# Where the second attention's weights and its first batch's pieces stand in the program

## The chip, the cores and the metric

The kernel runs on one core of a Trainium2 chip. Its time is the device time of one execution in microseconds (us), the median of several runs. The core has five engines with a queue each: PE multiplies matrices into PSUM, DVE, ACT and POOL work on vectors, SP issues transfers (DMA). PEld is PE's loading of the stationary operand. Each engine works through its own list of instructions in the order in which the list was written.

## The reference

Four batches of 512 rows of 128 numbers pass through a macaron: half a mixture of experts, linear attention, half a mixture of experts, half a block of six layers, softmax attention, and half a second block of the same six layers. The steps around the change are the end of the first block and the softmax attention:

```python
x = x + 0.5 * _L1_ffn_ref(_layernorm(x), ...)                 # six layers: local attention + gated FFN
x = x + _L1_attn_ref(_layernorm(x), W_Q, W_K, W_V, W_K_prime, W_O, alpha)
x = x + 0.5 * _L1_ffn_ref(_layernorm(x), ...)

def _L1_attn_ref(x, W_Q, W_K, W_V, W_K_prime, W_O, alpha):     # 16 heads of 8
    q, k, v, kp = (_heads(x @ W.T) for W in (W_Q, W_K, W_V, W_K_prime))
    out_std = softmax(q @ k.T / sqrt(8)) @ v
    out_p   = softmax(q @ kp.T / sqrt(8)) @ v
    return merge(alpha * out_std + (1 - alpha) * out_p) @ W_O.T
```

## The kernel before

The program is written in four parts: 0 the front (experts and linear attention), 1 the first block of layers, 2 the softmax attention, 3 the second block. Each piece of work is a Python generator whose steps are put on a list with a time (`Events.at`, L546); a step may name others that it must follow, and is then put just behind the latest of them, however early its own time was. A part is written out in the order of these times (`run`, L566). In parts 1 and 3 that order is kept on every engine (`manual_schedule`, L1387). In parts 0 and 2 a planner in the build orders the instructions, and it may move those of part 2 up among the last of part 1.

**The end of part 1.** A layer has two units of heads per batch (projections L299, norms L336 and L371, scores L434, softmax L457, values L416 and L482) and a gated FFN per batch (`Ffn`, L628). In the last layer of the block, the block's input is read back from DRAM into the one tile `xo` (`aside`, L731; L734 is the transfer), and `fadd` (L723) adds the FFN's output (L726) and then half of the sum to `xo` (L728). The time of `aside` (19.734, L611) puts the four pairs of `aside` and `fadd` behind everything else of part 1. Until its `fadd`, a batch's FFN output stays in one of the four PSUM banks "mm" (L68, L716).

**The softmax attention** (`l1_attn`, L1114).

- `weights` (L1119) loads four matrices of 128x128, one DMA each into `wr`, which has two buffers (L1122), and splits each into a high part on ACT (L854) and a low part on DVE (L855). W_O and alpha are loaded behind them.
- `prep` (L1153) makes one batch ready: a layer norm (L92 to L110), a transposition on PE (L860), a split (L854, L855), then for Q, K and K' three matmuls into a bank (`mm3`), three bf16 pieces of the result (`pc`, two buffers; ACT L1166, DVE L1167, ACT L1168, DVE L1169), and three DMAs that write them to DRAM (`pd`, L1173). V follows (L1177 to L1184).
- `first` (L1277) runs `prep(0)` and reads the pieces back, spread over heads, into the tiles of queries and keys (`load`, L1147: four DMAs each, L1151; `stack`, L1131, fills the unused rows).
- `slots` (L1326) then runs 32 units of four heads. A slot takes the row maxima of a new unit (16 matmuls L1200 into three banks in turn, each reduced on DVE, L1201), and, from the third slot on, scores, exponentials and averages of the unit that started two slots earlier (`LAG`, L1225 to L1241). `prep` of a later batch is fed in a step at a time (L1303).

Where they are put is said in four lines:

```python
ev.at(t0 - P["w"], (key, "w"), weights)                                   # L1339
ev.row(t0, P["dp"], names, first(), {names[0]: [(key, "w")] + ready[0:1], names[5]: memory[0:1]})
ready = l1_attn(..., ready=[((5, b), "fadd", 0) for b in range(4)],       # L1381
```

`ready` are the four `fadd` of the last layer: the attention's first step follows the first of them.

Of the kernel before, what the change touches and what calls it, by code (L numbers as in the profile page):

```python
# [6 lines left out]
F32 = mybir.dt.float32  # L7
# [84 lines left out]
def layernorm(g, x, outs, eps=1e-5):  # L92

    nc = g.nc
    st = tile_of(g, "lnst", [128, 4, 6], bufs=2)
    mv = tile_of(g, "lnmv", [128, 4, 2], bufs=2)
    for t in range(4):
        nc.vector.bn_stats(st[:, t, :], x[:, t, :])
        nc.vector.bn_aggr(mv[:, t, :], st[:, t, :])
    ve = tile_of(g, "lnve", [128, 4], bufs=2)  # L100
    rs = tile_of(g, "lnrs", [128, 4], bufs=2)
    nc.vector.tensor_scalar(ve, mv[:, :, 1], eps, None, ALU.add)
    rstd_newton(g, ve, rs, [128, 4], "ln")
    nb = tile_of(g, "lnnb", [128, 4], bufs=2)
    nc.vector.scalar_tensor_tensor(nb, mv[:, :, 0], -1.0, rs, ALU.mult, ALU.mult)
    for t in range(4):
        if t % 2:
            nc.scalar.activation(outs[:, t, :], x[:, t, :], AF.Identity, scale=rs[:, t:t + 1], bias=nb[:, t:t + 1])
        else:
            nc.vector.tensor_scalar(outs[:, t, :], x[:, t, :], mv[:, t, 0:1], rs[:, t:t + 1], ALU.subtract, ALU.mult)  # L110
# [747 lines left out]
def transpose4(g, ps, src):  # L858
    for t in range(4):
        g.nc.tensor.transpose(ps[:, t * 128:(t + 1) * 128], src[:, t, :], g.ident)  # L860
# [247 lines left out]
LAG = 2  # L1108


ATTN = dict(w=1.0, dp=0.06, s0=0.7, ds=0.384)


def l1_attn(g, w, x, ev, t0=0.0, blk=0, ready=None, memory=()):  # L1114
    nc = g.nc
    W, al = {}, tile_of(g, "al", [128, 2])
    tags = ["rtk", "rtk", "raw", "raw", "rtq", "rtq", "v", "v"]

    def weights():  # L1119
        for n in ("W_Q", "W_K", "W_K_prime", "W_V"):  # L1120
            t = g.wp.tile([128, 2, 128], FR, tag="wqk", name="s" + n, bufs=16)
            r = g.wp.tile([128, 128], F32, tag="wqkr", name="wr", bufs=2)  # L1122
            nc.sync.dma_start(r, w["L1_attn_" + n + "T"])
            split(g, t[:, 0, :], t[:, 1, :], r)
            W[n] = t
        W["O"] = g.wp.tile([128, 3, 128], F32, tag="w2", name="wo", bufs=1)[:, 0, :]
        nc.sync.dma_start(W["O"], w["L1_attn_W_OT"])
        nc.sync.dma_start(al[:, 0:1], w["L1_attn_alpha"].to_broadcast([128, 1]))
        nc.vector.tensor_scalar(al[:, 1:2], al[:, 0:1], -1.0, 1.0, ALU.mult, ALU.add)

# [20 lines left out]
            nc.sync.dma_start(t[hg // 2][0:SR, hg % 2], dram[(b, i)][:, :, :, hg].rearrange("a c d h n -> (a c d) h n"))  # L1151

    def prep(b):  # L1153
        y = g.wp.tile([128, 4, 128], F32, tag="wvraw", name="y", bufs=1)
        layernorm(g, x[b], y)
        p = bank(g, "mm", name="yT")
        transpose4(g, p, y)
        xT = g.wp.tile([128, 2, 512], FR, tag="rot", name="xT", bufs=3)
        split(g, xT[:, 0, :], xT[:, 1, :], p)
        yield  # L1160
        for i, n in enumerate(("W_Q", "W_K", "W_K_prime")):
            p = bank(g, "mm", name="qp")
            mm3(nc, p, W[n][:, 0, :], W[n][:, 1, :], xT[:, 0, :], xT[:, 1, :])
            pc = tile_of(g, "pt", [128, 3, 512], BF, "pc")
            t1 = g.wp.tile([128, 512], F32, tag="woraw", name="t1", bufs=1)
            nc.scalar.copy(pc[:, 0, :], p)  # L1166
            nc.vector.tensor_tensor(t1, p, pc[:, 0, :], ALU.subtract)  # L1167
            nc.scalar.copy(pc[:, 1, :], t1)  # L1168
            (nc.gpsimd if b else nc.vector).tensor_tensor(pc[:, 2, :], t1, pc[:, 1, :], ALU.subtract)  # L1169
            dram[(b, i)] = d = g.dr.tile([3, 3, 8, 4, 4, 512], BF, tag="pd", name="pd", bufs=4)  # L1170
            for c in range(3):
                dst = d[:, c] if i == 0 else d[c]
                nc.sync.dma_start(dst.rearrange("j d g h n -> (d g h) j n"), pc)  # L1173
            if i == 0 and b:
                load(b, i)
            yield
        p = bank(g, "mm", [128, 4, 16, 8], "vp")  # L1177
        for t in range(4):
            ts = slice(t * 128, (t + 1) * 128)
            mm3(nc, p[:, t], xT[:, 0, ts], xT[:, 1, ts], W["W_V"][:, 0, :], W["W_V"][:, 1, :])  # L1180
        if b == 0:
            vxs.extend(columns())
        vx = vxs[b % 2]
        nc.vector.tensor_copy(vx[:, :, 0:144].rearrange("p t (h c) -> p t h c", c=9)[:, :, :, 0:8], p)  # L1184
        st[b] = tile_of(g, "t2", [128, 4, 16, 8], name="O")
        yield
# [88 lines left out]
    extra = []  # L1275

    def first():  # L1277
        yield from prep(0)
        for i in range(3):
            (ks if i else qs).append(stack("k" if i else "q"))  # L1280
            load(0, i)
            yield
        qs.append(stack("q"))
        yield

    def pick(n):
        return units[n] if 0 <= n < len(units) else None

    def slot(n):
        if n == 0:  # L1290
            sb.extend([bank(g, t, name="S") for t in ("S", "n2", "mm")])
        if n < len(todo):
            units.append(Unit1(*todo[n]))
            if n % 8 == 3 and n < 24:
                extra.append(prep(n // 8 + 1))

        if n % 8 == 4 + LAG and n < 24:
            load(n // 8 + 1, 1)
        if n % 8 == LAG and 8 < n < 32:
            load(n // 8, 2)  # L1300
        U, P, A, B = (pick(n - k) for k in (0, 1, LAG, LAG + 1))
        for kt in range(4):
            if (kt in (0, 3) or not A) and extra:  # L1303
                if next(extra[0], 0) == 0:
                    extra.pop(0)
            for h in range(4):
                if U:
                    U.max(kt, h)
                if A:
                    A.score(kt, h)  # L1310
                if kt == 1 and h == 1 and P:
                    P.rows()
                if h == 3:
                    for c in range(2):
                        if kt and A:
                            A.mix(kt - 1, c)
                        if kt == 0 and B:
                            B.mix(3, c)
            if kt == 1 and B:
                B.norm()  # L1320
                if (B.br, B.hg) == (1, 3):
                    extra.insert(0, B.final())
            if U and kt == 3:
                U.pieces()
# [11 lines left out]

    P = ATTN
    key = ("at", blk)
    ev.at(t0 - P["w"], (key, "w"), weights)  # L1339
    names = [(key, "p", i) for i in range(9)]  # L1340
    ev.row(t0, P["dp"], names, first(), {names[0]: [(key, "w")] + (ready[0:1] if ready else []), names[5]: memory[0:1]})
    names = [(key, "s", i) for i in range(len(todo) + LAG + 2)]
    wait = {names[0]: [(key, "p", 8)] + list(memory)}
    for b in range(1, 4):
        wait[names[8 * b - 5]] = ready[b:b + 1] if ready else []
    ev.row(t0 + P["s0"], P["ds"], names, slots(), wait)
# [7 lines left out]
def macaron(tc, w, out):  # L1354
    with ExitStack() as ctx:
        g = G()
        g.nc, g.tc, g.ctx = tc.nc, tc, ctx
        nc = g.nc
        setup(g, w)
        x = [g.const.tile([128, 4, 128], F32, name=f"x{b}") for b in range(4)]  # L1360
        for b in range(4):
            nc.sync.dma_start(x[b], w["x"][b].rearrange("(t p) c -> p t c", p=128))
        dp = ctx.enter_context(tc.tile_pool(name="xo", bufs=1, space=bass.MemoryType.DRAM))
        xd = [dp.tile([128, 4, 128], F32, name=f"xd{b}") for b in range(4)]
        fill = setup_l1(g, w)

        F = Front(g, w, x)

        def side():
            F.mats()  # L1370
            fill()

        nc.scalar.preload_act_table_set("natural_log_exp_and_others")

        ev = Events()
        names = [("fr", i) for i in range(76)]
        ev.row(-13.0, .17, names, F.steps(side))
        ev.part = 1
        l1_ffn(g, w, x, ev, xd=xd, ready=names[-4:])
        ev.part = 2  # L1380
        ready = l1_attn(g, w, x, ev, PHASES[0], ready=[((5, b), "fadd", 0) for b in range(4)],  # L1381
                        memory=[((5, 1, 3), "vproj", 7, 1), ((5, 1, 3), "score", 1, 1, 0)])
        ev.part = 3
        l1_ffn(g, w, x, ev, PHASES[1], blk=1, xd=xd, ready=ready)
        for part in range(4):
            if part % 2:
                with tc.manual_schedule():  # L1387
                    ev.run(part)
            else:
                ev.run(part)  # L1390
        for b in range(4):
            nc.sync.dma_start(out[b].rearrange("(t p) c -> p t c", p=128), x[b])
# [19 lines left out]
```

## Time and profile before

| what | value |
|---|---|
| median of 3 runs | 4029.13 us (4029.07, 4029.13, 4037.15) |
| profiled execution: its own time | 4030.56 us |
| its span, first to last instruction | 4028.8 us |
| outside the span | 1.8 us |
| busy: PE, PEld | 3694.7 (92%), 2644.3 (66%) |
| busy: DVE, ACT, POOL | 3098.9 (77%), 2680.0 (67%), 2385.5 (59%) |
| mean granted clock of PE | 0.97 |

The profile is one execution, with a time for every instruction from the start of the span. Its page gives busy time by engine, the span in 40 slices, the chain of waits that ended last, and groups of instructions by source line. Further answers show a window of it: busy time by stage, instructions in order with the idle time before each and what ended it, waits by engine, and the chain of waits of that window. A "q" behind an engine's name marks its sequencer; for SP, these rows are DMA issues. PEclk is the share of full speed that PE was granted. The stages told of here lie in the stretch from 1920 to 2107 us.

### The profile page before, as it was taken

Reading aid. Unit: us, or ns where it says so; the run is one execution under the profiler, and the core shown is the slowest. Engines: PE = TensorE matmul, PEld = TensorE weight load, DVE = VectorE, ACT = ScalarE, POOL = GpSimd, SP = SyncE. Lnnn points to the kernel's source line nnn. Section 1 sums busy time; section 2 is a strip of 40 time slices with the busy share of each in tenths; the row PEclk is TensorE's granted clock in tenths of the full one; section 3 lists DMA queues with packets and bytes.
Section 4 is the critical chain, followed back from the end, with each engine's and each line's share of the span. In section 5 each row is a group of like instructions: output and inputs, shape, how many; then the busy total and the mean of one; then the engine's idle time right before and its main releaser. Section 6 shows DMA issues by size and latency. Waiting matters only on the chain.

```text
span 4028.8 us, 150401 instructions
## 1 busy us (share of the span) xinstructions
PE 3694.7 (92%) x66627; PEld 2644.3 (66%) x66628; DVE 3098.9 (77%) x5671; ACT 2680.0 (67%) x5226; POOL 2385.5 (59%) x2549
## 2 busy tenths in 40 slices
PE   7997979999999999999869999799999999999997
PEld 5765757777777777777533344477777777777765
DVE  5865778878888888888657778488887888888875
ACT  4654666777677677777526667667777777777763
POOL 2422447777877777786501111577777777777773
PEclk9997989999999999999969999899999999999998
DMA  2000024443444444343422220434344344444432
GB/s 62 22 16 11 16 59 95 87 99 79 100 85 90 92 86 93 82 101 78 88 84 73 73 73 12 97 78 95 83 88 100 78 100 85 92 88 87 95 72 47
DMA packets 139132, 306.18 MB, mean 76 GB/s; under 512 B 16584, under 2 KB 100944, under 8 KB 113456
## 3 DMA queue, kind: packets, MB, share of 16 engines
q0 software_dynamic: 31008, 202.40, 25.8%
q1 hardware_dynamic: 107472, 94.16, 8.1%
q8 instruction: 522, 8.55, 0.9%
q14 instruction: 130, 1.06, 0.1%
HBM read 77.49 MB, written 17.69 MB: 24 GB/s over the span
## 4 chain that ended last, share of the span: by engine, by line
PE 68%; DVE 8%; ACT 5%; POOL 3%; issue 3%; DMA 2%; SPq 0%; POOLq 0%; ACTq 0%; DVEq 0%
PE vps L425 10%; PE av L495 8%; PE S L452 6%; PE qkps L284 5%; PE qkps L285 4%; PE qkps L286 4%; PE R L404 3%; PE S L1200 3%; PE fout L719 3%; PE av L1237 3%; PE ST L1229 2%; POOL E L476 2%; PE n L344 2%; PE hps L284 2%; PE S L443 2%
## 5 line engine op out<-in xcount | busy, mean ns | idle before, releaser
L333 POOL TENSOR_TENSOR raw<-raw,rot 128x512 f32<-128x512 f32 x576 | 791.4, 1383 | 271.5 <-ACT sq L319 267.7
L425 PE MATMUL vps<-vo,xF 128*32 128x256 f32 x12288 | 742.7, 382 | 86.1 <-ACT vx L431 41.1
L425 PEld LDWEIGHTS vps<-vo,xF 128*32 128x32 f32 x12288 | 427.6, 110 | 329.6 <-ACT vx L431 69.8
L431 ACT COPY vx<-vps 128x512 f32<-128x512 f32 x768 | 421.6, 590 | 149.8 <-PE vps L425 148.2
L467 POOL TENSOR_TENSOR E<-E,rq 128x1024 f32<-128x1024 f32 x192 | 416.1, 2185 | 61.1 <-DVE E L464 49.8
L476 POOL TENSOR_TENSOR E<-E,smr 128x1024 f32<-128x1024 f32 x192 | 382.7, 2017 | 111.6 <-DVE smr L474 111.5
L316 ACT COPY raw<-qkps 128x512 f32<-128x512 f32 x576 | 334.1, 580 | 127.2 <-PE qkps L286 112.2
L991 POOL TENSOR_TENSOR h<-r,h 128x512 fp32r<-128x512 f32 x128 | 178.3, 1402 | 358.6 <-ACT r L990 285.2
L407 DVE TENSOR_TENSOR rtk<-rtk,R 128x512 f32<-128x512 f32 x384 | 253.9, 682 | 158.3 <-PE R L404 153.0
L1201 DVE TENSOR_REDUCE nm<-S 128x1 f32<-128x512 f32 x512 | 324.8, 682 | 64.8 <-PE S L1200 64.2
L319 ACT ACTIVATE sq<-raw 128x512 f32<-128x512 f32 x576 | 358.7, 631 | 20.5 <-PE n L344 5.1
L495 PE MATMUL av<-vx,pt 128*32 128x128 f32 x11904 | 367.4, 275 | 3.9 <-issue 3.7
L495 PEld LDWEIGHTS av<-vx,pt 128*32 128x32 f32 x11904 | 333.6, 110 | 48.4 <-issue 39.9
L284 PE MATMUL qkps<-xT,wqk 128*128 128x512 f32 x768 | 326.2, 425 | 32.8 <-ACT xT L276 22.4
L1230 ACT ACTIVATE E<-ST 128x512 f32<-128x512 f32 x512 | 273.6, 599 | 111.3 <-PE ST L1229 110.9
L462 DVE TENSOR_REDUCE mx<-S 128x16 f32<-128x1024 f32 x192 | 234.0, 1219 | 137.4 <-PE S L452 135.4
L452 PE MATMUL S<-rtk,rtq 64*32 64x64 f32 (+1 forms) x24576 | 290.7, 223 | 33.3 <-issue 32.9
L452 PEld LDWEIGHTS S<-rtk,rtq 64*32 64x32 f32 x24576 | 278.7, 105 | 51.1 <-issue 39.7
L285 PE MATMUL qkps<-xT,wqk 128*128 128x512 f32 x768 | 306.6, 399 | 1.1 <-POOL xT L279 1.1
L286 PE MATMUL qkps<-xT,wqk 128*128 128x512 f32 x768 | 306.0, 398 | 0.0
L324 DVE TENSOR_TENSOR rtk<-qkps,rot 128x512 f32<-128x512 f32 x384 | 251.0, 680 | 33.9 <-ACT raw L316 24.8
L472 DVE TENSOR_REDUCE sm<-E 128x16 f32<-128x1024 f32 x192 | 233.1, 1214 | 29.4 <-ACT E L469 29.3
(267 smaller groups left out, 8469.5 us busy)
## 6 DMA issues: line engine op xcount, KB each, us to landing
rtk<-raw POOLq DMA_DIRECT2D x192, 512.0 KB, 6.6
rtq<-raw POOLq DMA_DIRECT2D x192, 512.0 KB, 6.3
pd<-pc SPq DMA_DIRECT2D x36, 384.0 KB
wqkr<-in_L_ffn_Wqk SPq DMA_DIRECT2D x192, 64.0 KB
rot<-in_c_rot SPq DMA_DIRECT2D x24, 512.0 KB
k<-pd SPq DMA_DIRECT2D x32, 288.0 KB
r<-in_L_ffn_W SPq DMA_DIRECT2D x32, 256.0 KB
wvraw<-in_L_ffn_WvT SPq DMA_DIRECT2D x24, 256.0 KB
```

Source lines behind the costliest of these rows:

```text
L284: first = nc.tensor.matmul(out, lhsT=wh, rhs=xh, start=True, stop=False)
L285: nc.tensor.matmul(out, lhsT=wh, rhs=xl, start=False, stop=False)
L286: nc.tensor.matmul(out, lhsT=wl, rhs=xh, start=False, stop=True)
L316: nc.scalar.copy(raw, ps)
L319: nc.scalar.activation(sq, raw, AF.Square)
L333: nc.gpsimd.tensor_tensor(raw, raw, rot[:, 1, :], ALU.mult)
L425: nc.tensor.matmul(ps[p * 32:(p + 1) * 32, ww, :], lhsT=xF[:, t0:t0 + 32], rhs=g.vo[(self.l, self.hf, p // 2)][:, p % 2, :], start=True, s ...
L431: nc.scalar.copy(self.v[th][:, 2 * t:2 * t + 2, :], ps)
L452: nc.tensor.matmul(self.S[k][p * 32:(p + 1) * 32, ab, w * 64 + 64 - n:w * 64 + 64], lhsT=self.rt[1][rows, p, t0:t0 + 32], rhs=self.rt[0][r ...
L467: nc.gpsimd.tensor_tensor(E4, E4, self.rq[:, :, 8 * k:8 * k + 8].unsqueeze(3).to_broadcast([128, 2, 8, 64]), ALU.mult)
L476: nc.gpsimd.tensor_tensor(E, E, r.unsqueeze(2).to_broadcast([128, 16, 64]), ALU.mult)
L495: g.nc.tensor.matmul(self.av[ww * 32:(ww + 1) * 32, k, :], lhsT=self.pt[w // 8][:, ab, w % 8, role, :], rhs=self.v[src // 8][:, src % 8, a ...
```

## The change

The attention's weights and its first batch's projections and pieces are written in part 1, and so in its fixed order. `prep` stops more often (the new `yield "f"`); for the later batches the slots skip those stops. `names[:18]` are the steps of `prep(0)` up to the pieces of K'; V and the loads stay in part 2. The load of W_O moves from `weights` to the end of `first`. The weights now follow the eight projections of the last layer's unit (5, 0, 3).

```diff
-ATTN = dict(w=1.0, dp=0.06, s0=0.7, ds=0.384)
+ATTN = dict(w=2.4, early=1.6, dp=0.06, s0=0.7, ds=0.384)
...
-        W["O"] = g.wp.tile([128, 3, 128], F32, tag="w2", name="wo", bufs=1)[:, 0, :]
-        nc.sync.dma_start(W["O"], w["L1_attn_W_OT"])
...
         layernorm(g, x[b], y)
+        yield "f"
         p = bank(g, "mm", name="yT")
         transpose4(g, p, y)
+        yield "f"
         xT = g.wp.tile([128, 2, 512], FR, tag="rot", name="xT", bufs=3)
         split(g, xT[:, 0, :], xT[:, 1, :], p)
         yield
...
             mm3(nc, p, W[n][:, 0, :], W[n][:, 1, :], xT[:, 0, :], xT[:, 1, :])
+            yield "f"
             pc = tile_of(g, "pt", [128, 3, 512], BF, "pc")
             t1 = g.wp.tile([128, 512], F32, tag="woraw", name="t1", bufs=1)
             nc.scalar.copy(pc[:, 0, :], p)
+            yield "f"
             nc.vector.tensor_tensor(t1, p, pc[:, 0, :], ALU.subtract)
+            yield "f"
             nc.scalar.copy(pc[:, 1, :], t1)
+            yield "f"
...
         qs.append(stack("q"))
+        W["O"] = g.wp.tile([128, 3, 128], F32, tag="w2", name="wo", bufs=1)[:, 0, :]
+        nc.sync.dma_start(W["O"], w["L1_attn_W_OT"])
         yield
...
-                if next(extra[0], 0) == 0:
+                while (e := next(extra[0], 0)) == "f":
+                    pass
+                if e == 0:
                     extra.pop(0)
...
-    ev.at(t0 - P["w"], (key, "w"), weights)
-    names = [(key, "p", i) for i in range(9)]
-    ev.row(t0, P["dp"], names, first(), {names[0]: [(key, "w")] + (ready[0:1] if ready else []), names[5]: memory[0:1]})
+    names = [(key, "p", i) for i in range(23)]
+
+    ev.part -= 1
+    ev.at(t0 - P["w"], (key, "w"), weights, wait=memory[2:])
+    ev.row(t0 - P["early"], P["dp"], names[:18], gen := first(), {names[0]: [(key, "w")] + (ready[0:1] if ready else [])})
+    ev.part += 1
+    ev.row(t0, P["dp"], names[18:], gen, {names[18]: names[17:18], names[19]: memory[0:1]})
     names = [(key, "s", i) for i in range(len(todo) + LAG + 2)]
-    wait = {names[0]: [(key, "p", 8)] + list(memory)}
+    wait = {names[0]: [(key, "p", 22)] + list(memory[:2])}
...
-                        memory=[((5, 1, 3), "vproj", 7, 1), ((5, 1, 3), "score", 1, 1, 0)])
+                        memory=[((5, 1, 3), "vproj", 7, 1), ((5, 1, 3), "score", 1, 1, 0)] + [((5, 0, 3), "proj", c, 0) for c in range(8)])
```

In the built programs, the lists of the engines differ in these places alone:

- **The weights.** Before, the four ACT copies and DVE splits stand one by one among the projections of the last batch's first unit. After, all four stand in a row on ACT behind the table load that follows the second batch's gelu (L704), and in a row on DVE before the transposition of that unit's norm (L348). The scaling of one layer-6 matrix (ACT L192, POOL L194) moves a few instructions back.
- **The attention's first batch.** Before, on DVE, the four `fadd` and the layer norms of all batches alternate, then come the pieces. After, the order is: `fadd` of batch 0, its layer norm, the seven DVE instructions of its split and pieces, `fadd` of batch 1 with V's copy in it and half the `fadd` of batch 2 (L726), the statistics of batch 1, and then the row maxima. The rest of the `fadd` of batches 2 and 3 and of the layer norms of batches 1, 2 and 3 stands among the first 31 row maxima.
- **SP.** Before: reads of `xo` for batches 1 and 2, W_O, `xo` for batch 3, six writes of pieces, four loads of queries, three writes, eight loads of keys. After: W_O, six writes, four loads of queries, three writes, `xo` for batch 1, eight loads of keys, `xo` for batches 2 and 3.
- **PE.** The nine matmuls of Q, K and K' stand three by three for each, where the three first ones stood together.

## The prediction

> **What bounds the kernel now.** The page's slices come first: PE is busy 92% of the span, and its clock is full but for a dip in the middle.
>
> ```profile
> PE   7997979999999999999869999799999999999997
> ...
> PEclk9997989999999999999969999899999999999998
> ```
>
> The dip in the 21st slice (2014 to 2115 us) is the seam between the first block of layers and the attention. Busy time by stage shows what bounds each part of it:
>
> ```profile
> 2044.40:2061.70 17.30, 11.75 (x49) 9.85 (x49) 14.16 (x64) 5.17 (x16) 1.22 (x1) 0.61 0.17 50
> 2061.70:2082.00 20.30, 0.18 (x2) 0.04 (x1) 3.83 (x9) 1.82 (x3) 0.00 (x0) 0.57 0.86 263
> 2082.00:2101.10 19.10, 18.75 (x34) 3.76 (x35) 18.45 (x31) 0.26 (x1) 1.05 (x5) 0.50 0.38 92
> ```
>
> (Columns: length; PE, PEld, DVE, ACT, POOL; PE's clock; DMA share; GB/s.) First DVE is the fullest engine: adds and layer norms. Then only the DMAs work, at 263 GB/s: pieces are written to DRAM and read back. Then DVE is full again: 32 row maxima for the attention's first two slots. PE's 18.75 are matmuls that follow DVE's pace. The instructions in order of time, two engines' rows:
>
> ```profile
> 2061.69 5.05 SPq L1173 DMA_DIRECT2D pd<-pc  x6
> 2066.90 2.98 SPq L1151 DMA_DIRECT2D q<-pd  x4
> 2069.93 2.01 SPq L1173 DMA_DIRECT2D pd<-pc  x3
> 2071.98 9.94 SPq L1151 DMA_DIRECT2D k<-pd  x8
> 2082.00 12.74 PE L1200 MATMUL S<-k,q 96*128 96x512 bf16 x22 [20.12 <-DMA k<-pd]
> 2082.65 21.10 DVE L1201 TENSOR_REDUCE nm<-S 128x1 f32<-128x512 f32 x35 [13.30 <-PE S L1200]
> ```
>
> The first maximum's matmul waits 20.12 us for keys. From then on the maxima follow at 21.10 / 35 = 0.60 us each. The chain of waits, 120 us earlier, shows that the weights' loads are on the path where they stand now:
>
> ```profile
> 1922.50 0.74 DVE sW_Q L855
> 1923.24 0.60 DVE rtk L324
> 1923.84 0.71 DVE sW_K L855
> 1924.57 1.75 DMA wr<-in_L_attn_W_VT
> ...
> 1926.67 0.83 DVE sW_V L855
> 1927.50 1.15 DVE mx L462
> ```
>
> A DMA and splits are followed by mx, which has nothing to do with them but stands behind them on DVE.
>
> **The weights: what they give back.** Without the splits, the third rtk ends at 1923.8 instead of 1925.14. mx then waits only for PE's scores, which end at 1925.2: it starts at 1925.25 instead of 1927.42, 2.2 us earlier. PE's next matmul (hps) waits 4.96 us for a bank that DVE frees four instructions after mx, and gains the same: 1929.55 instead of 1931.74. PE's clock goes to half from 1931.53 to 1934.94, after a stretch of 3.41 us in which PE did nothing. With PE back 2.2 us earlier, over half of that stretch is busy, so I take full clock: hps 0.7 us for 1.6, 92 matmuls of av 2.7 for 3.6. The gain by the gelu is 2.2 + 1.7 = **3.9**. Bounds: 2.2 without the clock, 5.0 if all of PE's wait went.
>
> **What they cost in the new place.** In old times, ACT is free for them at 1944.30. The two copies of Q and K take 0.6. DVE splits Q and K from 1945.55 to 1946.95 (0.7 each). Only then are their buffers free for K' and V. From a split's end to the next copy the rows show 1.93 us (1923.24 to 1925.17) and 1.80 (1924.54 to 1926.34). So K' is copied at 1948.15, V at 1948.7 to 1949.0, and its split ends at 1950.0. Queued behind on ACT are the copies and squares of the last projections, both exponentials (L469) and the value copies (vx). The first exponential moves from 1945.90 to 1950.0, **4.1** later (0.5 of ACT's 4.7 falls on a wait that it had). DVE's row sums, POOL's product, DVE's transposition and ACT's copies that PE waits for at 1952.87 follow it. Bounds: 1.2 (four copies, if all waits were covered) and 4.7.
>
> PE meanwhile stops for 3.05 us, until the squares arrive. In its window of 3.41 us it is then busy about 28%. Rows: busy 0.66 of 3.41 (19%, a stop of 2.75 us) was followed by half clock, 1.86 of 3.41 (54%) by full. 19% is nearer, so I take half clock: three value tiles take twice 0.92, of which ACT's late copy hides all but **0.5**. Bounds 0 and 1.7.
>
> The Trainium skill says otherwise ("TensorE: Matmul & The Clock Gate", section on HAM oscillation): PE should have no idle gaps over about 3.4 us, so shorter ones are free. By that rule this term is 0 and the sum 0.5 less; the 2.75 us row disagrees, and it decides.
>
> The weights together: -3.9 + 4.1 + 0.5 = **+0.7**, bounds -3.8 (-5.0 + 1.2) and +4.2 (-2.2 + 4.7 + 1.7). Other edits there (the layer-6 scaling, 0.3 on ACT and 0.45 on POOL; alpha's DMA) are covered by the same waits; uncovered they cost 0.75.
>
> **The seam: the first keys come earlier.** `fadd` of batch 0 stands at the list's end whatever the new start time says, so `prep(0)` still starts at 2045.8. But its layer norm no longer waits behind two adds that wait for `xo`. Its statistics end at 2047.45 as before; then, at 0.2 a link, L87 to L105 end at 2048.95 (2053.35 before), L110 and L108 at 2049.8, PE's transposition at 2050.4, ACT's copy at 2051.0, DVE's split at 2051.7 (2056.90). One thing gets worse: batches 1 to 3 keep three of the four banks until their `fadd`, so Q's matmuls wait for the bank that the split frees: 2051.75 to 2053.4. Copy 0.58, difference 0.69, copy 0.62, difference 0.69, each plus 0.03: first piece complete at 2056.1, where it was 2061.66. That is **5.6** earlier. K and K' go one by one through that bank, 2.7 us each; the DMAs, still moving the first pieces, hide it.
>
> The six writes, four reads, three writes and the keys follow as before, with one read of `xo` (256 KB) now ahead of the keys: 0.7, from packets of 84 ns, eight on each of 16 engines. First maximum's matmul: 2082.0 - 5.6 + 0.7 = 2077.1, first maximum 2077.75 (2082.65).
>
> **The seam: what DVE has left to do.** Adds and norms that were done while the DMAs were awaited now stand among the first 31 maxima. By start-to-start in the rows: three adds 1.8, eight bn_stats 1.6, twelve bn_aggr 0.85, 15 small ones 1.2, L110 twice 0.5: **6.0**. DVE is full there, so nothing hides it. And L728 of batch 2 needs a read of `xo` that SP issues behind the eight loads of keys. Those end at 2091.26 - 5.6 + 0.7 = 2086.4, the read at 2087.1. DVE reaches L728 after nine maxima and 0.55, at 2083.7, and stops for **3.4**; behind it are the maxima, for which PE waits. Bounds: 0 (the read passes the keys) and 5.3 (it starts only when they are done and takes the 2.6 to 2.8 us that the rows show from issue to use). The last read is asked for 4.4 us before its use, so no stop.
>
> The 32nd maximum: 2077.75 + 32 x 0.60 + 6.0 + 3.4 = 2106.3, against 2101.8: **+4.5** (bounds +1.1, +6.4). From there both programs are alike.
>
> **Sum.** +0.7 + 4.5 = +5.2 us, on the profiled execution's 4030.56 (span 4028.8 and 1.8 outside). That run is 1.4 above the median; on the median, 4029.13 + 5.2 = 4034.3. The bounds add up to -2.7 and +10.6: 4026.4 to 4039.7. What this kernel's measurement can tell from no change is about 0.2%, 8.1 us. So the likeliest case is a small loss within it.
>
> **Rivals.**
> 1. *The row of four weights is not paid for* (slower). Place: ACT behind L704. If PE's clock stays full nowhere and only 2.2 come back, the weights cost up to 4.2, and with the seam's 4.5 it is +8.7: 4037.8. It decides once the weights cost over 3.6 net. For: ACT, DVE and PE all pass there in order. Against: the chain shows the same DMA waits on the path today.
> 2. *The first pieces come no earlier* (the change doesn't do what it says; slower). If bank and buffer waits eat the 5.6, maxima start at 2083.35 and all of DVE's extra comes on top: 4.5 + 5.6 + 0.7 = +10.8: 4039.9. For: one free bank, and the start that follows `fadd`. Against: the 4.4 us that the layer norm's L105 gains are a plain matter of order.
> 3. *Waits cover the extra work* (faster). If the weights cost their 1.2 alone and give back 5.0, and the read of `xo` and half of DVE's 6.0 fall into the wait for keys, it is -3.8 - 4.9 + 3.0 = -5.7; only with all of the 6.0 covered is it -8.7: 4020.4. Against: DVE's order puts most of it behind the first maximum.
>
> **How the numbers follow.** Forecast within 0.2%: 0.58 (its own range 4027 to 4037). Rival 1: 0.25. Rival 2: 0.10. Rival 3: 0.07. So faster 0.07, same 0.58, slower 0.25 + 0.10 = 0.35. Range 4026 to 4041: the bounds, up to rival 2; outside remain rival 3 and parts of 1 and 2.
>
> **What would show it.** mx (L462) some 2.2 us earlier and no half clock near 1931. ACT's K' copy idle for over 3 us behind L704. The first write of pieces some 5.6 us earlier against `fadd`, and the first S matmul some 4.9. A stop of about 3 us before L728 of the third batch, and 32 maxima that take 28.5 us instead of 19.1. I am wrong if the maxima's stretch grows by less than 5, or if the time from L704 to the next value copies is unchanged.

## The result, and the profile after

The changed kernel takes 4037.82 us (median of 20 runs, 4032.69 to 4043.31), the kernel before beside it 4032.04 us (20 runs, 4026.19 to 4037.20). The ratio is 1.0014, with a 95% interval of 1.0007 to 1.0020: some 5.6 us are lost, where the prediction had 5.2. The sum was right, but the experiments show that one of its terms, the gain at the clock, hardly came, and that another was too small. That 5.2 and 5.6 lie so close is partly luck: the interval reaches from 2.8 to 8.1 us, and misses of single terms cancel.

The profiled execution of the changed kernel has a span of 4038.6 us (its own time: 4040.45). Two profiles can differ by more than the medians do: identical code ahead of the change drifts by 1 to 3 us between the two traces, and behind it by as much. So the readings below are distances inside one profile. Line numbers are those of each kernel's own file; in the changed kernel they are a few higher than in the one before (L1205 is the maxima's matmul, L1206 the maximum, L1178 the writes of pieces).

The page's slices differ from those of before in two digits of the clock alone: 8 for 7 in the fourth slice, and 5 for 6 in the dip.

**The weights' new place.** The rows of ACT in order of time, first of the kernel before, then of the changed one:

```profile
1943.02 1.28 ACT L704 ACT_TABLE_LOAD   x1
...
1945.90 1.04 ACT L469 ACTIVATE E<-E 128x1024 f32<-128x1024 f32 x1
```

```profile
1942.08 1.28 ACT L704 ACT_TABLE_LOAD   x1
1943.37 0.30 ACT L854 CAST sW_Q<-wr 128x128 fp32r<-128x128 f32 x1
...
1946.64 0.30 ACT L854 CAST sW_K_prime<-wr 128x128 fp32r<-128x128 f32 x1 [2.77 <-DMA wr<-in_L_attn_W_K_primeT]
...
1948.58 1.04 ACT L469 ACTIVATE E<-E 128x1024 f32<-128x1024 f32 x1
```

The third matrix waits for its buffer and its DMA, as forecast. The exponential (L469) starts 6.50 us behind the start of the table load (L704), where it was 2.88: 3.6 us later (forecast 4.1). PE's rows show the wait that it gains and the one that it gets, and DVE's the start of mx. Again first the kernel before:

```profile
1927.42 1.21 DVE L462 TENSOR_REDUCE mx<-S 128x16 f32<-128x1024 f32 x1
...
1931.74 0.80 PE L284 MATMUL hps<-xnT,w 128*128 128x512 f32 x1 [4.96 <-DVE rtq L324]
...
1933.32 3.59 PE L495 MATMUL av<-vx,pt 128*32 128x128 f32 x92
```

```profile
1924.99 1.23 DVE L462 TENSOR_REDUCE mx<-S 128x16 f32<-128x1024 f32 x1 [1.21 <-PE S L452]
...
1929.32 0.80 PE L284 MATMUL hps<-xnT,w 128*128 128x512 f32 x1 [2.80 <-DVE rtq L324]
...
1930.90 5.06 PE L495 MATMUL av<-vx,pt 128*32 128x128 f32 x92
...
1949.69 1.93 PE L425 MATMUL vps<-vo,xF 128*32 128x256 f32 x16 [3.61 <-DVE rtq L324]
```

The first stop is 2.80 us instead of 4.96, and mx starts at 1924.99 instead of 1927.42: 2.4 us won at mx and 2.2 at PE's stop. But the 92 matmuls of av behind it take 5.06 us. Before they took 3.59; in e4 below, at full clock throughout, 2.82.

**The seam.** The rows of SP's queue and of PE:

```profile
2060.44 5.07 SPq L1178 DMA_DIRECT2D pd<-pc  x6
2065.67 2.98 SPq L1149 DMA_DIRECT2D q<-pd  x4
2068.70 1.79 SPq L1178 DMA_DIRECT2D pd<-pc  x3
2070.53 1.18 SPq L734 DMA_DIRECT2D xo<-xd  x1
2071.76 8.73 SPq L1149 DMA_DIRECT2D k<-pd  x8
2081.82 12.36 SPq L734 DMA_DIRECT2D xo<-xd  x2
```

```profile
2081.80 7.22 PE L1205 MATMUL S<-k,q 96*128 96x512 bf16 x12 [12.15 <-DMA k<-pd]
```

`fadd` of batch 0 starts at 2048.92 here and at 2044.40 before. Counted from it, the first write of pieces comes after 11.52 us instead of 17.29, and the first S matmul after 32.88 instead of 37.60: 5.8 and 4.7 us earlier. Then DVE, in order of time:

```profile
2087.69 0.69 DVE L1206 TENSOR_REDUCE nm<-S 128x1 f32<-128x512 f32 x1
2093.12 0.69 DVE L728 SCALAR_TENSOR_TENSOR x<-x,xo 128x512 f32<-128x512 f32 x1 [4.74 <-DMA xo<-xd]
```

This is the stop for batch 2's `xo`, whose read is the first of the last two on SP, issued behind the eight loads of keys. Busy time by stage (from `fadd` to the first write, to the first S matmul, to the end of the 32nd maximum) puts it together:

```profile
2048.92:2060.44 11.52, 8.58 (x34) 7.24 (x34) 6.62 (x21) 3.09 (x7) 1.22 (x1) 0.65 0.02 6
2060.44:2081.80 21.36, 4.77 (x17) 3.57 (x17) 5.75 (x11) 2.41 (x4) 0.00 (x0) 0.50 0.88 264
2081.80:2112.22 30.42, 19.64 (x36) 3.97 (x36) 25.44 (x75) 2.55 (x10) 1.06 (x5) 0.50 0.31 75
```

In the last stage DVE (third pair) has 75 instructions where it had 31 in the stage shown of before. The 32 maxima take 29.80 us instead of 19.22.

### The profile page after: what moved, and what is told of

It is laid out like the page before. It is cut to its first block, busy times and chain, and to the rows that moved or that the text cites. A ratio compares the mean times of both kernels' runs of the same rounds, so it can differ in the third digit from the quotient of the medians.

```text
span 4038.6 us, 150394 instructions
## 1 busy us (share of the span) xinstructions
PE 3696.8 (92%) x66628; PEld 2646.7 (66%) x66628; DVE 3098.7 (77%) x5671; ACT 2686.8 (67%) x5226; POOL 2388.9 (59%) x2549
## 4 chain that ended last, share of the span: by engine, by line
PE 68%; DVE 8%; ACT 5%; issue 3%; POOL 3%; DMA 2%; SPq 0%; POOLq 0%; ACTq 0%; DVEq 0%
PE vps L425 10%; PE av L495 8%; PE S L452 6%; PE qkps L284 5%; PE qkps L285 4%; PE qkps L286 4%; PE fout L719 3%; PE R L404 3%; PE av L1242 3%; PE ST L1234 3%; PE S L1205 2%; PE n L344 2%; POOL E L476 2%; PE hps L284 2%; PE hps L286 2%
## 5 line engine op out<-in xcount | busy, mean ns | idle before, releaser
L333 POOL TENSOR_TENSOR raw<-raw,rot 128x512 f32<-128x512 f32 x576 | 792.0, 1384 | 271.3 <-ACT sq L319 267.4
L407 DVE TENSOR_TENSOR rtk<-rtk,R 128x512 f32<-128x512 f32 x384 | 254.2, 683 | 158.2 <-PE R L404 153.0
L1206 DVE TENSOR_REDUCE nm<-S 128x1 f32<-128x512 f32 x512 | 326.9, 684 | 51.4 <-PE S L1205 50.8
L462 DVE TENSOR_REDUCE mx<-S 128x16 f32<-128x1024 f32 x192 | 234.1, 1219 | 143.4 <-PE S L452 142.0
L472 DVE TENSOR_REDUCE sm<-E 128x16 f32<-128x1024 f32 x192 | 233.2, 1215 | 29.1 <-ACT E L469 29.1
```

The costliest lines, as they stand in the source:

```text
L333: nc.gpsimd.tensor_tensor(raw, raw, rot[:, 1, :], ALU.mult)
```

## The experiments

Three groups of runs (e1 to e4, e5 to e7, and e8 with one run), each on another chip, with the kernel before beside it. That kernel's own median differed from group to group (4019.47 and 4027.19 us; 4023.10 in the one run beside e8), so only ratios count. As a second measure, distances between fixed DVE instructions of each profile follow; these are one execution each.

**e1: the weights alone are moved.** The kernel before, with this edit and W_O's load moved as in the change:

```diff
-    ev.at(t0 - P["w"], (key, "w"), weights)
+    ev.part -= 1
+    ev.at(t0 - 2.4, (key, "w"), weights, wait=memory[2:])
+    ev.part += 1
```

> Only the weights stand in the new place (as in the changed kernel); the pieces, the adds and the row maxima stand as before. My theory gives the weights +0.7 us (bounds -3.8 and +4.2): about 4032.7 on a median before of 4032.0. First rival (the row of four weights is not paid for): +4, about 4036, of the changed kernel's 5.8 us. Second rival (only the seam costs): 0. In the trace: mx (L462) some 2.2 us earlier against the kernel before; first exponential (L469) behind the second batch's gelu 3.6 to 4.1 us later than without the weights there; a stop of PE of 3 to 3.6 us there, then half clock. If the clock after the first stop is a matter of chance between executions, this profile shows the half clock near 1931 us over one window, two or none, and the gain at the second mx is anywhere from 0.7 to 3.9. The maxima's stretch is as before: 32 in 19.1 us, no stop before L728.

Measured: 4020.33 against 4019.47, ratio 1.0004 (0.9996 to 1.0013), some 1.6 us. That is inside the bounds, near my +0.7, and its interval reaches from -1.6 to +5.2, so the rival's +4 isn't excluded by the times alone. The first exponential starts 6.53 us behind L704, PE stops for 3.65 us. The half clock near 1924 lasts one window. The 32 maxima take 19.22.

**e2: the first batch's steps alone are moved.** The changed kernel, with each weight's load, copy and split as three steps, tied to the projections among which they stood before:

```diff
-    ev.at(t0 - P["w"], (key, "w"), weights, wait=memory[2:])
+    for i, n in enumerate(gens):
+        put(n, 0, U, ("proj", (0, 0, 0, 2)[i], (0, 0, 3, 3)[i]), (-2.0, -1.9, 6e-7, 6e-7)[i])
+        put(n, 1, *((U, ("proj", (0, 2, 4)[i], 1), 2e-7) if i < 3 else (V, ("soft", 0, 0), -4e-7)))
+        put(n, 2, *((U, ("proj", (0, 2)[i], 3), 3e-7) if i < 2 else (V, ("soft", 0, 0), (-5e-7, -3e-7)[i - 2])))
```

(`U` is the unit (5, 0, 3), `V` is (5, 1, 2); `put` sets a step's time just beside that of a step of these. Alpha and W_O stay where the change has them.)

> Only the first batch's projections and pieces are moved (as in the changed kernel); the weights are loaded and split one by one among the projections, where they stood before. My theory gives the seam +4.5 us (bounds +1.1 and +6.4), the profile of the changed kernel +5.6: about 4037 on a median before of 4032.0. Rival (the weights cost all): 0. In the trace: until the seam as before (mx behind the splits of V, half clock near 1931 us as it falls out); first write of pieces 5.6 us earlier against fadd, first S matmul 4.7 to 4.9 earlier, a stop of 4 to 5 us before L728 of the third batch, and 32 maxima in 29 us instead of 19.1.

Measured: 4024.54 against 4019.47, ratio 1.0011 (1.0003 to 1.0020), some 4.4 us: the forecast's size. The two parts add up to the whole (1.6 + 4.4 against 5.6). The stop is 3.45 us here (4 to 5 expected), 32 maxima take 28.50.

**e3: the adds go between the steps.** The changed kernel; the read of `xo` and `fadd` of batches 1, 2 and 3 follow the layer norm, the first difference of Q and the first difference of K of batch 0:

```diff
+    for (k, a, f), n, m in zip(ev.late, (ready[0], names[0], names[5]), (names[0], names[5], names[10])):
+        put(k, "aside", a, n, 4e-7)
+        put(k, "fadd", f, m, 2e-7)
```

> The changed kernel, but the reads of xo and the adds (fadd) of batches 1 to 3 are written between the steps of the first batch's projections: the three reads go out before the pieces' writes, and DVE has the adds and nearly all of the layer norms behind it before the first row maximum. My theory: the loss of the seam is DVE's moved work (6.0 us) and the stop for xo (4.7) among the maxima, not the early pieces themselves. Then 48 maxima stand in a row, 32 take 19.1 us, no stop before L728; the first piece comes some 2 us later than in the changed kernel (three adds and statistics stand before it), the keys' reads are no longer behind a read of xo (0.7): first S matmul 3 to 4 us earlier against fadd than before. Seam -3 instead of +5: some 8 to 9 us less than the changed kernel, 4029 where that has 4037.8. Rival (half clock of PE, or the early pieces' DMAs, make the maxima's stretch long, whatever DVE has to do): 32 maxima still take over 25 us, and the time stays within 2 us of the changed kernel.

Measured: 4014.72 against 4019.47, ratio 0.9989 (0.9980 to 0.9998): 4.4 us less than before, and some 10 less than the changed kernel. SP's rows and DVE's, in order of time:

```profile
2047.59 5.16 SPq L734 DMA_DIRECT2D xo<-xd  x2
2053.03 5.81 SPq L1183 DMA_DIRECT2D pd<-pc  x6
...
2063.86 9.46 SPq L1154 DMA_DIRECT2D k<-pd  x8
```

```profile
2074.02 21.10 DVE L1211 TENSOR_REDUCE nm<-S 128x1 f32<-128x512 f32 x35 [12.24 <-PE S L1210]
```

All reads of `xo` go out before the pieces. DVE has done its adds and all of the layer norms but the last step (L110) of two batches when the keys arrive; then 35 maxima follow in 21.10 us, as before. The first write comes 12.18 us behind `fadd`, only 0.66 later than in the changed kernel (some 2 expected), since DVE had holes there: in the changed kernel's stage it is busy 6.62 of 11.52 us. PE is at half clock during these maxima (its clock reads 0.50 in this stage of e3, as it does in the changed kernel), and they take 19.22 us all the same. So neither the half clock nor the early pieces made the stretch long: it was DVE's work and the stop, which e3 takes away together.

**e4: own buffers for the third and fourth matrix.** The changed kernel, with:

```diff
-            r = g.wp.tile([128, 128], F32, tag="wqkr", name="wr", bufs=2)
+            r = g.wp.tile([128, 128], F32, tag="wr" if n in ("W_K_prime", "W_V") else "wqkr", name="wr", bufs=2)
```

> The changed kernel, but the loads of the third and fourth weight matrix have two buffers of their own, so that all four DMAs go out together. My theory: in the new place it is the wait for the third matrix (ACT idle 2.8 us behind the table load, 0.3 for the fourth) that delays the first exponential (L469), the value copies and then PE. Without it the four copies follow each other in 1.2 us, L469 starts 2.5 to 3.1 us earlier against L704, PE's stop there falls from 3.6 us to about 0.6, and PE's clock stays full behind it: 3 to 4 us less than the changed kernel, about 4034. Rival (the wait is covered by what PE and POOL wait for anyway): no change within 1 us, and the landmarks at the end of part 1 (the first fadd) stand as late as in the changed kernel.

Measured: 4023.05 against 4019.47, ratio 1.0001 (0.9993 to 1.0010), against 1.0014 of the changed kernel: some 5 us less (forecast 3 to 4), though the two intervals overlap. e7 against e1, below, is the same step, and as large; there, too, the intervals overlap. ACT's rows:

```profile
1934.01 0.29 ACT L854 CAST sW_K<-wr 128x128 fp32r<-128x128 f32 x1
1934.21 0.29 ACT L854 CAST sW_K_prime<-wr 128x128 fp32r<-128x128 f32 x1
...
1935.76 1.04 ACT L469 ACTIVATE E<-E 128x1024 f32<-128x1024 f32 x1
```

The four copies follow each other, and L469 starts 3.24 us behind L704 instead of 6.50. PE's stop there falls to 0.45 us. So at the exponential the wait for the third matrix is what the new place costs; the row of four copies and splits itself costs 0.36.

**e5, e6, e7: what the parts are worth together.** e5 is e3 and e4 together; e6 is e3 with the weights where e2 has them; e7 is e1 with e4's buffers.

> The adds between the first batch's steps, and own buffers for the third and fourth weight matrix, together. If weights and seam are separate costs, they add up: from the landmark ahead of the weights to the first fadd 3 us less than before, from that fadd to the 48th row maximum 5 to 6 less: some 8 to 9 us under the kernel before (ratio 0.998). Rival (what is won early is waited for later, as at the keys' DMAs): about as the adds alone, ratio 0.999.

> The adds between the first batch's steps, with the weights one by one among the projections as before. Seam alone: 5 to 6 us under the kernel before (ratio 0.9986); up to the first fadd no change, but for the half clock's chance of 1.5 us. Rival (the early seam needs the weights' new place): no gain.

> The weights alone in the new place, with own buffers for the third and fourth; pieces and adds as before. My theory: 3 us less than before (ratio 0.9993), of which 2.2 to 2.5 are at mx (L462) and up to 1.5 at the half clock near 1931; copies and splits cost 0.3 to 1.2. If the half clock falls there by chance of its windows (3.41 us long), this profile has none, one or two of them between the first and the second mx, and that distance is 9.7, 11.2 or 12.4 us accordingly. Rival (the row of four still costs what the move gives back): within 1 us of before.

Measured beside 4027.19: e5 4020.53, ratio 0.9981 (0.9972 to 0.9989); e6 4022.11, ratio 0.9985 (0.9976 to 0.9993); e7 4023.74, ratio 0.9991 (0.9983 to 0.9999). That is 7.7, 6.0 and 3.6 us less than before. The seam's gain alone is 6.0, the weights' alone 3.6, both together 7.7 (8 to 9 expected): most of it adds up, within what the intervals allow. e5 has the lowest ratio, under both kernels. Its profile has the seam's half of the forecast, 5.7 us from the first `fadd` to the 48th maximum, but of the weights' 3 us up to that `fadd` only 0.5. e7's profile shows no gain by the 48th maximum (below the table): it had two windows of half clock, and took 1.5 us longer from the row sum to `fadd`. That single profile speaks for its rival and the median of 12 runs for my theory; the profiled run (4027.86 us) was one of the slowest of the 12.

**e8: alpha ahead of the weights.** The changed kernel, with alpha's load and operation as the first of `weights` instead of the last.

> The changed kernel, with alpha's load and its DVE operation ahead of the four weights instead of behind them. In the changed kernel that operation waits 0.70 us for its DMA and stands on DVE ahead of the transposition and the product (L324) that PE's stop of 3.61 us ends with. If alpha is the last link there, as the chain of waits has it, the stop falls by 0.7 to about 2.9 us, while ACT still waits 2.8 us for the third matrix and L469 still starts 5.2 us behind L704. If the squares that follow the fourth copy on ACT end the stop as well, it stays at 3.6. In one profile the time itself tells nothing at this size.

Measured in one profile:

```profile
1942.07 1.49 PE L425 MATMUL vps<-vo,xF 128*32 128x256 f32 x12 [2.69 <-DVE rtq L324]
```

PE's stop falls from 3.61 to 2.69 us: alpha was the last link there. ACT still waits 2.92 us for the third matrix, L469 starts 6.43 behind L704, and the sum (L472) behind it is as late as ever (11.95 us behind the second mx, 12.04 in the changed kernel). PE's stop and ACT's are two effects of one row, and ACT's is the one that delays the softmax.

**All profiles side by side.** Distances in us, worked out from the starts of DVE's instructions: from the first mx (L462; at 1927.42 us in the kernel before) to the second (1938.56 there); from there to the row sum (L472); from the row sum to `fadd`; from `fadd` to the first maximum; length of 32 maxima, to the end of the last; DVE's stop for batch 2's `xo`. "Half" is PE's half clock between the two mx.

| kernel | mx to mx | half | to sum | to fadd | to max | 32 max | stop |
|---|---|---|---|---|---|---|---|
| before | 11.14 | 3.41 | 8.42 | 97.42 | 38.25 | 19.22 | 0.81 |
| changed | 12.63 | 6.83 | 12.04 | 99.27 | 33.50 | 29.80 | 4.74 |
| e1 weights | 11.28 | 3.41 | 12.06 | 98.12 | 37.34 | 19.22 | 0.93 |
| e2 pieces | 12.11 | 6.83 | 8.40 | 97.05 | 32.11 | 28.50 | 3.45 |
| e3 adds | 11.37 | 3.41 | 12.10 | 99.16 | 33.17 | 19.22 | 0 |
| e4 buffers | 9.71 | 0 | 8.76 | 98.01 | 32.16 | 28.36 | 3.33 |
| e5 both | 11.38 | 3.41 | 8.78 | 98.47 | 33.50 | 19.23 | 0 |
| e6 adds, old weights | 12.38 | 6.83 | 8.41 | 97.58 | 32.67 | 19.23 | 0 |
| e7 weights, buffers | 12.63 | 6.83 | 8.77 | 98.89 | 37.48 | 19.23 | 0.76 |

The landmark ahead of the weights is an earlier mx, at 1873.78 us in the kernel before. From it to the end of the 48th maximum it is 240.35 us in e7 (before 239.85, e5 233.62, changed 250.25).

## Why the prediction was right, and where it was wrong

**What the weights give back, first half: right.** mx comes 2.4 us earlier (2.5 counted from the landmark) and PE's stop falls from 4.96 to 2.80: the 2.2 of the forecast.

**Second half, the clock: wrong.** The step that failed is "over half of that stretch is busy, so I take full clock", the 1.7 of the 3.9. In the changed kernel's profile it was a loss of 1.5. The rows by stage, cut at the clock's own windows of 3.41 us; first the changed kernel, then e5, then e4 (second number: PE's busy time; the 1.00 or 0.50 near the end: its clock):

```profile
1925.31:1928.72 3.41, 1.21 (x6) 0.66 (x4) 3.38 (x5) 1.22 (x2) 1.64 (x2) 1.00 0.02 5
1928.72:1932.13 3.41, 2.81 (x27) 1.98 (x30) 1.14 (x2) 1.06 (x4) 2.89 (x3) 0.50 0.58 115
1932.13:1935.55 3.42, 3.42 (x70) 3.11 (x65) 0.39 (x2) 0.69 (x2) 2.10 (x2) 0.50 0.95 192
```

```profile
1923.87:1927.28 3.41, 1.14 (x11) 0.72 (x14) 2.81 (x5) 0.86 (x3) 1.22 (x3) 1.00 0.00 0
1927.28:1930.69 3.41, 3.41 (x72) 3.34 (x67) 0.39 (x2) 1.62 (x5) 3.41 (x3) 0.50 0.97 192
```

```profile
1917.97:1921.38 3.41, 1.94 (x41) 1.24 (x26) 2.98 (x4) 1.48 (x3) 2.36 (x2) 1.00 0.02 5
1921.38:1924.79 3.41, 2.10 (x47) 1.68 (x51) 1.86 (x4) 1.03 (x3) 2.17 (x3) 1.00 0.31 62
1924.79:1928.20 3.41, 3.41 (x194) 3.06 (x187) 0.52 (x3) 0.71 (x2) 2.76 (x2) 1.00 1.02 204
```

The same stop of 2.78 to 2.80 us falls in one window for the most part (busy 1.21 and 1.14 of 3.41, then half clock; in the changed kernel for two windows) or is cut in two by a window's edge (1.94 and 2.10, full clock). Within an execution the edges keep one grid: in the kernel before, the half windows that start at 1931.53 and 1996.38 us are 19 times 3.413 apart. Where the grid lies differs from execution to execution: the last edge before the first mx is 0.4 us ahead of it in e4, 1.4 in e5 and 3.1 in e7, whose weights stand alike. I had measured the busy share in the window of the trace of before, which the next execution does not have. Over the seven profiles with the weights in the new place (e8's is 11.37, with one window), mx to mx is 11.48 on average; over the three with them in the old place it is 11.88. So in these profiles, which scatter from 9.71 to 12.63, the term is worth some 0.4 on average and not 1.7. Each half window costs what the table shows: 9.71 us with none, 11.1 to 11.4 with one, 12.1 to 12.6 with two.

In the stretch from 1905 to 2005 us of all ten profiles, every window at full clock with PE busy for at most 43% was followed by half clock (19 of 19), of the 20 from 45 to 61% four, and none above.

The Trainium skill ("TensorE: Matmul & The Clock Gate") was weighed in the prediction with its rule on gaps (section on HAM oscillation): no idle gaps of PE over about 3.4 us. That shorter gaps are free, as the prediction read it, these stops of 2.80 us contradict. Its Part 1 has the rule that these rows bear out: the window of about 3.4 us is free-running and does not start with the work, so the same kernel can differ from run to run.

**What the weights cost: right at the exponential.** Forecast 4.1, measured 3.6, all but 0.4 of it the wait for the third matrix (e4, e7: 8.76 and 8.77 to the sum, before 8.42). The forecast had 0.7 for a split; in the new place it took 0.28 to 0.29, and the matrix's load can go out that much earlier. The second half clock, after the stop of 3.61 us, is there in the changed kernel, from 1949.20. In e1 a window's edge cuts the stop of 3.65 us in two (45 and 49% busy), and the clock stays full: this term, too, hung on where the edges lie. From the row sum to the next product (L407) it is 0.7 us longer than before in the changed kernel, 0.6 in e3 and 0.15 in e8, all three with that half clock, and no longer than before in e1; but e4, e5 and e7, without it, have 0.4. The forecast of 0.5 fits, and is not shown. Alpha was not covered: the prediction's "covered by the same waits" is wrong on PE, by 0.9 us (e8), without effect on the softmax.

**The weights' sum.** In the changed kernel's profile they cost 4.5 us by the first `fadd` (-2.5, +1.5, +3.6, and +1.9 from the sum to `fadd`, of which 0.7 is at that clock). In times they cost 1.6 (e1); the changed kernel against e2 gives 1.2 and e3 against e6 1.6, with intervals of 3 us and more either way. The forecast was 0.7. So the price was nearer my first rival's than my own in one execution, for the reason that this rival names: the clock stays full nowhere. In times it was not so. But up to the first `fadd` all four profiles with the two buffers lie above the forecast: 4.5, 2.0 (e1), 3.5 (e3) and 3.0 (e8) over before. What the sum lacked is the stretch from the row sum to `fadd`, for which it had the clock's 0.5 alone: in all seven profiles with the weights in the new place it is longer than before, by 0.6 to 1.9 us (1.2 on average), while e2 and e6 have -0.4 and +0.2. In the changed kernel 1.1 of the 1.9 arises about 1990 us, where clock windows and short stops of PE also differ from profile to profile. What causes this stretch was not settled.

**The seam: right, term by term.** First pieces 5.6 earlier (measured 5.8), first S matmul 4.9 (4.7). DVE's moved work 6.0: the maxima's growth less the stop is 29.80 - 19.22 - 4.74 = 5.8, and e2, e4 and e8 give the same 5.8. The stop 3.4: 4.74, 3.45, 3.33 and 4.55. Together, by the 32nd maximum, +5.8 in the changed kernel's profile, +3.1 in e2's, +3.0 in e4's and +4.7 in e8's, where 4.5 was forecast; by times, 4.4. The scatter is in the DMAs: the stop differs, and the stage from the first write to the first S matmul took 21.4 us in the changed kernel, 20.1 in e2.

**The rivals.** "The first pieces come no earlier" fell at the first row. "Waits cover the extra work" is what e3 had to be built for: the same work does fit into the wait for the keys, once it is written there. The prediction had it that only DVE's order stood against this, and e3 shows it.

## What to carry to other kernels

An early start of a chain pays only if the work that stood beside it stays in the wait: here the first keys came 4.7 us earlier, and 5.8 us of adds and norms, with a stop for a read queued behind the keys' loads, fell among the maxima. Written between the chain's own steps, the same work cost the chain 0.7 us and nothing later. And when loads are moved together, count their buffers: two buffers for four matrices made a wait of 2.8 us, which two more took away.

## What the runs showed of the hardware

**DVE beside POOL.** A split of 128x128 on DVE took 0.69 to 0.83 us in the kernel before, and 0.28 to 0.29 in the changed one. The rows of DVE in e2 (old place):

```profile
1920.32 0.74 DVE L1130 TENSOR_TENSOR sW_K_prime<-wr,sW_K_prime 128x128 fp32r<-128x128 f32 x1 [0.32 <-ACT sW_K_prime L1128]
1921.47 0.29 DVE L1130 TENSOR_TENSOR sW_V<-wr,sW_V 128x128 fp32r<-128x128 f32 x1 [0.41 <-ACT sW_V L1128]
```

While the first of these ran, POOL was at a product of rows (L333, to 1920.91); during the second it did nothing. The first split ended at 1921.06, 0.15 us behind that product, and each of the ten slow splits (four in the kernel before, three each in e2 and e6) ended 0.14 to 0.15 us behind the POOL product that ran when it began. That fits a split that waits until the product is over, better than one that runs at a lower rate. In all ten profiles, the splits beside POOL's work, all in the old place, took 0.69 to 0.85 us, and those without it 0.28 to 0.29, in the old place (e2, e6) as in the new. The prediction had priced the new place with 0.7 each. The Trainium skill ("Advanced Engine Details and Errata", GPSIMD Details) says that POOL shares a read and a write interface with DVE and conflicts with its instructions that have two SBUF inputs. These splits have two, and the rows agree.

**A read that takes longer to issue.** The one read of `xo` between the pieces and the keys took SP 1.18 us to issue in the changed kernel (1.00 in e2, 0.93 in e4, 0.69 in e8), where an issue of the same transfer takes 0.32 to 0.35 in the kernel before. Why was not tried.
